# The steady round of a cross-attention kernel, its statements in another order

## The chip, the cores and the metric

The kernel runs on one core of a Trainium2 chip. The metric is the device time of one execution in microseconds (us). The time before is 1385.47 us, the median of three runs (1383.31 to 1385.71).

## What is computed

There are B = 64 sequences of 256 rows. Each has text rows of 512 values (`H_l`, the input x) and context rows of 384 values (`H_a`, the input ctx_768). All is float32. In the reference, cut to what matters:

```python
text_p  = einsum('bld,dh->blh', H_l, W_text)  + b_text
audio_p = einsum('bsd,dh->bsh', H_a, W_audio) + b_audio
Q = layer_norm(text_p, g1, beta1)
K = layer_norm(audio_p, g2, beta2)
alpha = softmax(einsum('blh,bsh->bls', Q, K) / sqrt(512))
H_hyper = einsum('bls,bsh->blh', alpha, audio_p)
H_hyper = einsum('blh,hk->blk', H_hyper, W_out) + b_out
return layer_norm(H_hyper + H_l, g_out, beta_out)
```

## The kernel before

**A pipeline of rounds.** One loop runs over the sequences, `for b in range(B - 2)`. Rounds 3 to 60 take its first branch (`if fast:`, L1315), the steady round; that branch is one list of some 140 calls, written out by hand, and it is all that the change touches. In it eight sequences are under way at once:

- b + 4 and b + 3: blocks of x and c are loaded (`load_c`, `load_x`), turned on VectorE (`turn_x`, `turn_c`), and sums of their blocks are made on GpSimd (`SumX` L293, `Sides` L321; each `.add(1)` is one GpSimd sum).
- b + 2: `k2` and `q2`, the projections to K and Q. Their variances, then `normalise` on ScalarE, then `store` to DRAM and `fetch` back in blocks of 32 x 32, so that the rows can be turned.
- b + 1: `k[b + 1].turn` and `q[b + 1].turn` on VectorE and `affine_keys` on ScalarE (gain and shift by column); `key_step(0)` to `(2)`, sums of key blocks on GpSimd.
- b: `at`: `affine_queries`, `query_step(0)` to `(3)` on GpSimd, the scores, their maxima, exponentials and the division, `store_e`.
- b - 1 and b - 2: `last` and `old`: the exponentials come back (`fetch_e`, `turn_e`) and are multiplied with the context (`context_one`, `context_two`); `y = old.o` multiplies with the output weights, and `plus_...`, `last_10`, `last_11`, `last_01`, `last_00` add x and leave the rows with their totals.
- b - 3: `settled`: the last layer norm. `totals` (L983, two GpSimd instructions on one column, the means `nm`), `deviation(0)`, `(1)` and `last_deviation` on ScalarE, then on VectorE, for each of two row tiles t, `shift(t)` (L1141, row plus mean, times gain) and `settle(t)` (L1152, row times 1/deviation, plus shift). These four each read two operands of 128 x 512 from SBUF and write SBUF. `done.store` sends the rows out.

**Fewer products.** The matrix products are written as block schemes with fewer multiplications, at the price of sums: `Fork` (L701) makes q by seven products, `Thirds` (L534) makes k and y by fifteen each, the scores take seven parts. So an accumulator in PSUM is used again and again: a product is added, ScalarE copies the state, VectorE writes the difference into another accumulator, more products follow. `k2` and `y` use the same accumulators M, L, T, U and N one after the other, and the same rooms in SBUF (`n1`, `t`, `m`, `n`, `u`, `d`); R and q1 to q3 are those of `Fork`. Some steps of the chain of `Thirds`: products `one` into N; `copy_n1` (ScalarE); `start_t` (VectorE, T from N); `three` into T; `copy_t`; `two` into M; `start_l0`, `start_l1` (L from M and t); `four`; `take_m`, `start_u` (U from M); `five`; `copy_n`, `copy_u`; `leave_middle`, `leave_ends`, `leave`; `middle_d`, `middle_sum` (GpSimd). `seed` puts the bias into M, `Fork.seed` into R. For the scores, `score_part(5)` writes where `add_p7(0)` has read, and `score_part(3)` where `add_p7(1)` has read.

**What sets the order.** The kernel is under a manual schedule: each engine executes its instructions in the order in which the statements issue them, and waits by one semaphore per engine for what other engines produce. So a list of statements is five queues: TensorE (PE), VectorE (DVE), ScalarE (ACT), GpSimd (POOL) and SyncE (SP). All loads and stores stand in SP's queue, and an issue there waits for its data and blocks those behind it. Buffers are few: the pool `once` has one of each tile (`kr`, `qr`, `zsum`, `ksum`, `qsum`, `e`), `work`, `blk`, `xin` and `cin` have two.

Helper lines that the profile names: L548 products of `Thirds`, L721 of `Fork`, L867 of the scores, L945 of the context; L532 the VectorE sums; L343 sums of `Sides` (`csum`, `zsum`), L314 of `SumX`, L849 `key_step`, L852 `query_step`, L990 `totals`; L518 affine, L1008 `deviation`, L479 and L787 `normalise` of k and q; L511 `turn` of k, L73 the loads in blocks, L489 `store` of k and q.

Of the kernel before, what the change touches and what calls it, by code (L numbers as in the profile page):

```python
# [22 lines left out]
def kernel(  # L23
# [20 lines left out]
    B, L, D = x.shape  # L44
# [24 lines left out]
    def squares(dst, src):  # L69

        v = src.rearrange("(b j) (q f) -> q j b f", j=SQ, q=NQ)
        for q in (0, 2, 1, 3):
            nc.sync.dma_start(dst[q * SQ : (q + 1) * SQ], v[q])  # L73
# [7 lines left out]
    def load_c(b):  # L81
        cq = blk.tile([P, S // SQ, DA // NQ], F32, tag="cq", name=f"cq_{b}")
        squares(cq, c[b])
        blocks[b] = [cq]

    def load_x(b):
        xq = blk.tile([P, L // SQ, D // NQ], F32, tag="xq", name=f"xq_{b}")
        squares(xq, x[b])
        blocks[b].append(xq)
# [5 lines left out]
    def load_x_rows(b):  # L95
        x_rows[b] = xin.tile([P, LT, D], F32, tag="x", name=f"x_{b}")
        nc.sync.dma_start(x_rows[b], x[b].rearrange("(t p) d -> p t d", p=P))

    def load_c_rows(b):
        c_rows[b] = cin.tile([P, ST, DA], F32, tag="c", name=f"c_{b}")  # L100
        nc.sync.dma_start(c_rows[b], c[b].rearrange("(t p) d -> p t d", p=P))
# [308 lines left out]
    def rstd_beside(var, n, by=1.0):  # L410

        log = small.tile([P, n], F32, tag=f"log{n}", name="log")
        nc.scalar.activation(log, var, AF.Ln, bias=eps, scale=by)
        r = small.tile([P, n], F32, tag=f"rstd{n}", name="rstd")
        nc.scalar.activation(r, log, AF.Exp, scale=-0.5)  # L415
        return [r[:, t : t + 1] for t in range(n)]
# [109 lines left out]
    def scales_of(a, b, var):  # L526

        r = rstd_beside(var, 4)
        a.r, b.r = r[:2], r[2:]
# [171 lines left out]
    class Fork(Projection):  # L701

        R, q1 = fork[0][:, :H2], fork[0][:, H2:]
        q2, q3 = fork[1][:, :H2], fork[1][:, H2:]
# [465 lines left out]
    def turn_x(b):  # L1170
        xT = work.tile([P, DC, L], F32, tag="xT", name=f"xT_{b}")
        turn(xT, blocks[b][1], DC)
        return xT

    def turn_c(b):
        cT = work.tile([P, AC, S], F32, tag="cT", name=f"cT_{b}")
        turn(cT, blocks[b][0], AC)
        return cT
# [7 lines left out]
    q, k, xT, cT, xs, cs, att = {}, {}, {}, {}, {}, {}, {}  # L1186
# [48 lines left out]
    wt_blocks = weight_sums(wt_sb, DC // 2, "wtsum")  # L1235
# [73 lines left out]
    for b in range(B - 2):  # L1309
        at = att[b] = att.get(b) or Attention(b)  # L1310
        settled, old, last = att.pop(b - 3, None), att.get(b - 2), att.get(b - 1)
# [3 lines left out]
        if fast:  # L1315
            k2 = k[b + 2] = Thirds("k", b + 2, cs.pop(b + 2), wa_blocks, ba_sb, ba_delta)
            q2 = q[b + 2]
            x_old = x_rows[b - 2]

            var = small.tile([P, 4], F32, tag="var4", name="var")  # L1320
            last.fetch_e()
            k2.one()
            old.context_two(0); old.context_two(1)
            if b + 4 < B: load_c(b + 4)
            k2.copy_n1()
            k2.start_t()
            old.copy_two()
            settled.totals()
            at.affine_queries(1)
            cT[b + 3] = turn_c(b + 3)  # L1330
            at.affine_queries(0)
            q2.six()
            old.start_products(n=1)
            y = old.o
            k2.three()
            k2.copy_t()
            k2.two()
            k2.start_l0()
            at.affine_queries(2)
            old.zsides.add(1)  # L1340
            q2.seven()
            k2.start_l1()
            at.query_sums()
            at.query_step(0)
            old.zsides.add(1)
            at.affine_queries(3)
            settled.deviation(0)
            k2.four()
            xT[b + 3] = turn_x(b + 3)
            k2.take_m()  # L1350
            q2.after_seven()
            settled.deviation(1)
            at.query_step(1)
            old.zsides.add(1)
            k2.start_u()
            k2.five()
            k2.copy_n()
            k2.copy_u()
            at.open_scores()
            q2.start_q3()  # L1360
            old.zsides.add(1)
            at.query_step(2)
            y.one()
            y.copy_n1()
            q2.step_r()
            q2.five()
            k2.leave_ends()
            old.zsides.add(1)
            y.seed()
            k2.leave_middle()  # L1370
            settled.last_deviation()
            k[b + 1].turn([0])
            k2.leave()
            k[b + 1].turn([1])
            y.start_t()
            at.score_part(1, 7)
            k2.square(var[:, 2:], [0])
            at.copy_p1()
            q2.after_five()
            y.two()  # L1380
            at.copy_p7()
            q[b + 1].turn()
            old.zsides.add(1)
            y.three()
            y.copy_t()
            load_x_rows(b - 1)
            y.start_l1()
            q2.four()
            q2.two()
            at.query_step(3)  # L1390
            cs[b + 3] = Sides(cT.pop(b + 3), "csum").add(0)
            cs[b + 3].add(1)
            last.turn_e()
            y.start_l0()
            k2.middle_d()
            settled.shift(1)
            at.score_part(6)
            at.add_p7(0)
            q2.three()
            settled.settle(1)  # L1400
            att[b + 1] = Attention(b + 1)
            att[b + 1].affine_keys(0)
            y.four()
            y.take_m()
            at.score_part(5)
            x_new = SumX(xT.pop(b + 3))
            x_new.add(1)
            att[b + 1].affine_keys(2)
            y.start_u()
            x_new.add(1)  # L1410
            y.five()
            k2.middle_sum()
            q2.square(var[:, :2], [1])
            at.add_p7(1)
            load_c_rows(b)
            att[b + 1].affine_keys(1)
            k2.square(var[:, 2:], [1])
            if done: done.store()
            done = settled
            y.plus_ends(x_old)  # L1420
            at.score_part(4)
            y.last_11()
            q2.square(var[:, :2], [0])
            cs[b + 3].add(1)
            at.score_part(3)
            att[b + 1].affine_keys(3)
            x_new.add(1)
            scales_of(q2, k2, var)
            at.score_part(2)
            k2.normalise([0])  # L1430
            k2.normalise([1])
            q2.normalise([0])
            k2.seed()
            cs[b + 3].add(1)
            if b + 4 < B: att[b + 1].key_sums()
            if b + 4 < B: att[b + 1].key_step(0)
            y.plus_middle(x_old, 1)
            if b + 4 < B: load_x(b + 4)
            cs[b + 3].add(1)
            y.plus_n0()  # L1440
            if b + 4 < B: att[b + 1].key_step(1)
            at.maxima()
            q2.normalise([1])
            Fork.seed()
            k2.store()
            last.context_one()
            settled.shift(0)
            at.exponentials([0])
            at.exponentials([1])
            y.last_10()  # L1450
            at.reciprocals()
            last.copy_one()
            y.plus_middle(x_old, 0)
            at.divide_e([0])
            q2.store()
            q3 = q[b + 3] = Fork(b + 3, x_new.of, wt_blocks)
            q3.one()
            x_new.add(1)
            y.last_01(x_old)
            k2.fetch()  # L1460
            cs[b + 3].add(1)
            at.divide_e([1])
            cs[b + 3].add(1)
            y.last_00()
            cs[b + 3].add(1)
            Fork.clear()
            q3.after_one()
            at.store_e()
            if b + 4 < B: att[b + 1].key_step(2)
            q2.fetch()  # L1470
            settled.settle(0)

            continue
        if b + 4 < B and b not in (1, 2):
# [6 lines left out]
        k2 = k[b + 2] = Thirds("k", b + 2, cs.pop(b + 2), wa_blocks, ba_sb, ba_delta)  # L1481
        if b < 3:
            q[b + 2] = Fork(b + 2, xs.pop(b + 2), wt_blocks)
        q2 = q[b + 2]
# [128 lines left out]
        var = small.tile([P, 4], F32, tag="var4", name="var")  # L1613
# [86 lines left out]
        if three and b > 1:  # L1700
            q3 = q[b + 3] = Fork(b + 3, xs.pop(b + 3), wt_blocks)
# [33 lines left out]
    settled, old, last = att[B - 5], att[B - 4], att[B - 3]  # L1735
    at = att[B - 2]
# [135 lines left out]
```

## Time and profile before

| What | Value |
|---|---|
| median of three runs | 1385.47 us (1383.31 to 1385.71) |
| the profiled execution's own time | 1384.61 us |
| its span, first to last instruction | 1382.8 us |
| PE busy in the span | 1360.8 us (98%) |
| PEld (weight loads) | 1245.9 us (90%) |
| DVE, ACT, POOL busy | 1195.5, 1166.7, 1159.2 us (86, 84, 84%) |
| packets of SP's queue, share of the 16 DMA engines' time | 80.9% |
| granted TensorE clock | 0.998 |

The profile is one execution, taken by the hardware profiler. A busy PE is not a PE at its peak: matmuls are pipelined and their ends are modelled, so a short wait between two of them can lie inside busy time. Every float32 matmul stands in the trace as two records, so a product of one matmul is "x2" and a pair of products is "x4". In the time lines, a row has the start in us, the length in us, the engine, the line, the operation, the tiles (output <- inputs), the shapes and the count of instructions merged into it; in brackets stands the idle time before it and what ended that. A group's row ends in busy time and mean ns. A row of the view by one line or one tile has min / median / max in ns.

### The profile page before, as it was taken

What the parts mean: (1) busy time and instruction counts of PE and PEld (TensorE: products, weight loads), DVE (VectorE), ACT (ScalarE), POOL (GpSimd) and SP (SyncE); (2) the same over time, 40 slices, a digit from 0 to 9 for tenths busy, and PEclk for the clock granted to TensorE, in tenths of its full rate; (3) what the DMA queues carried; (4) which work ended last, traced back from release to release, by engine and by line L of the source; (5) the groups of instructions that cost most, each with busy time, mean ns of one, the idle gap of its engine ahead of it and who ended that gap; (6) DMA issues with size and microseconds to landing.
All of it is one profiled execution on the core that took longest, in us unless ns stands there. A gap on an engine that the chain in (4) does not pass through costs nothing.

```text
span 1382.8 us, 28546 instructions
## 1 busy us (share of the span) xinstructions
PE 1360.8 (98%) x8125; PEld 1245.9 (90%) x8125; DVE 1195.5 (86%) x2733; ACT 1166.7 (84%) x3188; POOL 1159.2 (84%) x1838
## 2 busy tenths in 40 slices
PE   9999999999999999999999999999999999999997
PEld 5788999999999999999999999999999999999985
DVE  6758898899889899889998898998998988998857
ACT  5688888888888888888888888888888888888874
POOL 5669889889899889889888889889888898898844
PEclk9999999999999999999999999999999999999999
DMA  9787888888888888888888888888888888888772
GB/s 215 212 230 197 249 236 233 252 237 229 251 235 238 248 237 234 252 237 235 246 243 234 246 243 234 245 246 233 244 243 229 248 231 242 247 235 245 218 217 92
DMA packets 449107, 322.15 MB, mean 233 GB/s; under 512 B 153781, under 2 KB 381621, under 8 KB 448950
## 3 DMA queue, kind: packets, MB, share of 16 engines
q1 hardware_dynamic: 448854, 320.20, 80.9%
q8 instruction: 65, 1.06, 0.3%
q14 instruction: 92, 0.75, 0.2%
q10 hardware_dynamic: 96, 0.13, 0.0%
HBM read 203.57 MB, written 116.65 MB: 232 GB/s over the span
## 4 chain that ended last, share of the span: by engine, by line
PE 89%; DMA 3%; ACT 3%; DVE 3%; SPq 1%; issue 1%; DVEq 0%; POOL 0%; ACTq 0%
PE ps_f L721 26%; PE ps_m L548 16%; PE ps_sc L867 14%; PE ps_z L945 11%; PE ps_n L548 10%; PE ps_u L548 8%; PE ps_l L548 5%; DMA qd<-qr 1%; SPq L73 1%; DMA wo<-in_L_xattn_W_out_dram 1%; ACT junk L451 1%; DMA kd<-kr 0%; ACT junk L777 0%; DVE yr L1144 0%; DMA wt<-in_L_xattn_W_text_dram 0%
## 5 line engine op out<-in xcount | busy, mean ns | idle before, releaser
L1144 DVE SCALAR_TENSOR_TENSOR yr<-yr,nm,go 128x512 f32<-128x512 f32 x124 | 201.5, 1625 | 1.0 <-ACT junk L1025 1.0
L721 PE MATMUL ps_f<-wtsum,xsum 128*128 128x256 f32 x756 | 193.6, 379 | 0.5 <-DVE ps_f L532 0.5
L945 PE MATMUL ps_z<-eT,c 128*128 128x256 f32 x768 | 186.6, 379 | 0.2 <-ACT e L896 0.2
L343 POOL TENSOR_TENSOR csum<-csum,cT 128x256 f32<-128x256 f32 x310 | 178.6, 586 | 0.9
L343 POOL TENSOR_TENSOR zsum<-zsum,zT 128x256 f32<-128x256 f32 x305 | 170.5, 568 | 5.3
L849 POOL TENSOR_TENSOR ksum<-kT 128x512 f32<-128x512 f32 x58 | 73.9, 1274 | 97.9 <-ACT rstd L415 88.1
L721 PEld LDWEIGHTS ps_f<-wtsum,xsum 128*128 128x128 f32 x756 | 137.9, 190 | 15.3 <-DVE ps_f L532 1.2
L945 PEld LDWEIGHTS ps_z<-eT,c 128*128 128x128 f32 x768 | 138.5, 190 | 14.0 <-ACT e L896 0.6
L518 ACT ACTIVATE kT<-kT,columns 128x256 f32<-128x256 f32 x256 | 144.5, 593 | 2.6 <-DVE kT L511 1.5
L518 ACT ACTIVATE qT<-qT,columns 128x256 f32<-128x256 f32 x256 | 139.7, 596 | 2.2 <-DVE qT L76 2.2
L721 PE MATMUL ps_f<-wt,xT 128*128 128x256 f32 x504 | 129.4, 379 | 0.6 <-ACT ps_f L713 0.6
L532 DVE TENSOR_TENSOR ps_l<-ps_m,t 128x171 f32<-128x171 f32 x248 | 83.4, 336 | 52.7 <-PE ps_m L548 44.5
L867 PE MATMUL ps_sc<-kT,qT 128*128 128x128 f32 x928 | 122.3, 275 | 0.0
L867 PEld LDWEIGHTS ps_sc<-kT,qT 128*128 128x128 f32 x928 | 119.2, 192 | 3.0
L867 PE MATMUL ps_sc<-ksum,qsum 128*128 128x128 f32 x696 | 111.2, 282 | 0.4 <-DVE ps_sc L532 0.4
L721 PEld LDWEIGHTS ps_f<-wt,xT 128*128 128x128 f32 x504 | 95.5, 190 | 14.4 <-ACT ps_f L713 1.1
L867 PEld LDWEIGHTS ps_sc<-ksum,qsum 128*128 128x128 f32 x696 | 96.1, 191 | 11.4 <-DVE ps_sc L532 5.2
L990 POOL TENSOR_SCALAR nm<-totals 128x1 f32<-128x1 f32 x124 | 70.1, 580 | 38.7 <-DVE yr L691 38.7
L343 POOL TENSOR_TENSOR csum<-cT 128x256 f32<-128x256 f32 x124 | 96.6, 779 | 6.6 <-DVE cT L76 6.6
L343 POOL TENSOR_TENSOR zsum<-zT 128x256 f32<-128x256 f32 x122 | 72.6, 595 | 25.7 <-ACT zT L964 25.7
L314 POOL TENSOR_TENSOR xsum<-xT 128x256 f32<-128x256 f32 x124 | 88.3, 735 | 1.2 <-DVE xT L76 1.2
L1153 DVE SCALAR_TENSOR_TENSOR yr<-yr,rstd,beo 128x512 f32<-128x512 f32 x120 | 85.8, 717 | 0.0
(265 smaller groups left out, 4164.8 us busy)
## 6 DMA issues: line engine op xcount, KB each, us to landing
kd<-kr SPq DMA_DIRECT2D x64, 512.0 KB, 3.1
kq<-kd SPq DMA_DIRECT2D x256, 128.0 KB, 3.1
qd<-qr SPq DMA_DIRECT2D x64, 512.0 KB, 3.2
qq<-qd SPq DMA_DIRECT2D x256, 128.0 KB, 3.5
xq<-in_x_dram SPq DMA_DIRECT2D x252, 128.0 KB, 6.2
x<-in_x_dram SPq DMA_DIRECT2D x63, 512.0 KB, 4.5
out_dram<-yr SPq DMA_DIRECT2D x62, 512.0 KB, 6.2
cq<-in_ctx_dram SPq DMA_DIRECT2D x252, 96.0 KB, 2.4
```

Of the source, the lines that this page charges most:

```text
L314: self.engine.tensor_tensor(*step)
L343: nc.gpsimd.tensor_tensor(*step)
L518: nc.scalar.activation(self.T[:, k, :], self.T[:, k, :], AF.Identity, bias=bet[:, k : k + 1], scale=gam[:, k : k + 1],)
L532: nc.vector.tensor_tensor(o, i0, i1, op)
L548: nc.tensor.matmul(place, lhsT=self.sides.of[n], rhs=self.weights[n], start=(n == 14), stop=True, skip_group_check=True,)
L721: nc.tensor.matmul(place, lhsT=side, rhs=w, start=False, stop=True, skip_group_check=True)
L849: nc.gpsimd.tensor_tensor(*self.ksteps[n])
L867: nc.tensor.matmul(self.place(t, m), lhsT=self.qsides[n][:, c], rhs=self.ksides[n][:, c], start=False, stop=True, skip_group_check=True,)
L945: nc.tensor.matmul(ps, lhsT=c_rows[self.b][:, s, bass.ts(j, P)], rhs=self.eT[:, s, :], start=start, stop=(s == ST - 1), skip_group_check=True,
L990: nc.gpsimd.tensor_scalar(self.nm[:, j : j + 1], t[:, 0, j : j + 1], t[:, 1, j : j + 1], -1.0 / D, ALU.add, ALU.mult)
L1144: nc.vector.scalar_tensor_tensor(row, row, self.nm[:, t : t + 1], go_sb, ALU.add, ALU.mult)
L1153: nc.vector.scalar_tensor_tensor(self.y[:, t, :], self.y[:, t, :], self.r[t], beo_sb, ALU.mult, ALU.add)
```

## The change

The statements of the steady round stand in another order. None is added, removed or altered; nothing outside the branch is touched. Minus is the order before, plus the order after (unmarked lines kept their place in the comparison):

```diff
 x_old = x_rows[b - 2]
 
 var = small.tile([P, 4], F32, tag="var4", name="var")
-last.fetch_e()
 k2.one()
-old.context_two(0); old.context_two(1)
-if b + 4 < B: load_c(b + 4)
 k2.copy_n1()
 k2.start_t()
+xT[b + 3] = turn_x(b + 3)
+old.context_two(0); old.context_two(1)
 old.copy_two()
-settled.totals()
-at.affine_queries(1)
-cT[b + 3] = turn_c(b + 3)
-at.affine_queries(0)
-q2.six()
 old.start_products(n=1)
 y = old.o
+q2.seven()
+at.affine_queries(1)
 k2.three()
 k2.copy_t()
+at.open_scores()
+settled.totals()
 k2.two()
+at.affine_queries(0)
+q2.after_seven()
+k2.start_l1()
 k2.start_l0()
+settled.deviation(0)
+q2.six()
+last.fetch_e()
+old.zsides.add(1)
+q2.start_q3()
+settled.deviation(1)
+k2.four()
 at.affine_queries(2)
-old.zsides.add(1)
-q2.seven()
-k2.start_l1()
+at.affine_queries(3)
+q2.step_r()
+k2.take_m()
 at.query_sums()
 at.query_step(0)
 old.zsides.add(1)
-at.affine_queries(3)
-settled.deviation(0)
-k2.four()
-xT[b + 3] = turn_x(b + 3)
-k2.take_m()
-q2.after_seven()
-settled.deviation(1)
-at.query_step(1)
 old.zsides.add(1)
 k2.start_u()
 k2.five()
+settled.shift(0)
+q2.five()
+old.zsides.add(1)
 k2.copy_n()
 k2.copy_u()
-at.open_scores()
-q2.start_q3()
-old.zsides.add(1)
-at.query_step(2)
+settled.last_deviation()
+if b + 4 < B: load_c(b + 4)
+at.query_step(1)
 y.one()
 y.copy_n1()
-q2.step_r()
-q2.five()
+k[b + 1].turn([0])
+k2.leave_middle()
 k2.leave_ends()
+k2.leave()
+q2.after_five()
 old.zsides.add(1)
+k2.middle_d()
+at.score_part(1, 7)
+k[b + 1].turn([1])
 y.seed()
-k2.leave_middle()
-settled.last_deviation()
-k[b + 1].turn([0])
-k2.leave()
-k[b + 1].turn([1])
+at.copy_p7()
+at.query_step(2)
 y.start_t()
-at.score_part(1, 7)
+q2.three()
+at.copy_p1()
+old.zsides.add(1)
+at.query_step(3)
+y.three()
+q2.four()
+q[b + 1].turn()
+at.score_part(6)
+att[b + 1] = Attention(b + 1)
+att[b + 1].affine_keys(0)
+k2.middle_sum()
 k2.square(var[:, 2:], [0])
-at.copy_p1()
-q2.after_five()
+load_x_rows(b - 1)
+x_new = SumX(xT.pop(b + 3))
+x_new.add(1)
 y.two()
-at.copy_p7()
-q[b + 1].turn()
-old.zsides.add(1)
-y.three()
+cT[b + 3] = turn_c(b + 3)
+at.add_p7(0)
 y.copy_t()
-load_x_rows(b - 1)
+att[b + 1].affine_keys(3)
 y.start_l1()
-q2.four()
-q2.two()
-at.query_step(3)
+att[b + 1].affine_keys(1)
 cs[b + 3] = Sides(cT.pop(b + 3), "csum").add(0)
 cs[b + 3].add(1)
-last.turn_e()
+cs[b + 3].add(1)
 y.start_l0()
-k2.middle_d()
+q2.two()
 settled.shift(1)
-at.score_part(6)
-at.add_p7(0)
-q2.three()
-settled.settle(1)
-att[b + 1] = Attention(b + 1)
-att[b + 1].affine_keys(0)
+q2.square(var[:, :2], [1])
+q2.square(var[:, :2], [0])
+at.score_part(5)
+k2.square(var[:, 2:], [1])
+cs[b + 3].add(1)
+att[b + 1].affine_keys(2)
+if b + 4 < B: att[b + 1].key_sums()
+if b + 4 < B: att[b + 1].key_step(0)
+at.add_p7(1)
+settled.settle(0)
+scales_of(q2, k2, var)
 y.four()
-y.take_m()
-at.score_part(5)
-x_new = SumX(xT.pop(b + 3))
+k2.normalise([0])
+at.score_part(3)
+at.score_part(2)
 x_new.add(1)
-att[b + 1].affine_keys(2)
-y.start_u()
-x_new.add(1)
-y.five()
-k2.middle_sum()
-q2.square(var[:, :2], [1])
-at.add_p7(1)
-load_c_rows(b)
-att[b + 1].affine_keys(1)
-k2.square(var[:, 2:], [1])
 if done: done.store()
 done = settled
+q2.normalise([0])
+y.take_m()
+y.start_u()
+q2.normalise([1])
+cs[b + 3].add(1)
+cs[b + 3].add(1)
+last.turn_e()
+k2.normalise([1])
+at.score_part(4)
+x_new.add(1)
+at.maxima()
+at.exponentials([0])
+y.five()
+last.context_one()
+Fork.seed()
+q3 = q[b + 3] = Fork(b + 3, x_new.of, wt_blocks)
+q3.one()
+cs[b + 3].add(1)
+if b + 4 < B: load_x(b + 4)
 y.plus_ends(x_old)
-at.score_part(4)
-y.last_11()
-q2.square(var[:, :2], [0])
-cs[b + 3].add(1)
-at.score_part(3)
-att[b + 1].affine_keys(3)
 x_new.add(1)
-scales_of(q2, k2, var)
-at.score_part(2)
-k2.normalise([0])
-k2.normalise([1])
-q2.normalise([0])
-k2.seed()
-cs[b + 3].add(1)
-if b + 4 < B: att[b + 1].key_sums()
-if b + 4 < B: att[b + 1].key_step(0)
+at.exponentials([1])
+k2.store()
+load_c_rows(b)
 y.plus_middle(x_old, 1)
-if b + 4 < B: load_x(b + 4)
-cs[b + 3].add(1)
+last.copy_one()
+q2.store()
 y.plus_n0()
 if b + 4 < B: att[b + 1].key_step(1)
-at.maxima()
-q2.normalise([1])
-Fork.seed()
-k2.store()
-last.context_one()
-settled.shift(0)
-at.exponentials([0])
-at.exponentials([1])
 y.last_10()
+k2.fetch()
+y.last_11()
 at.reciprocals()
-last.copy_one()
+at.divide_e([1])
 y.plus_middle(x_old, 0)
 at.divide_e([0])
-q2.store()
-q3 = q[b + 3] = Fork(b + 3, x_new.of, wt_blocks)
-q3.one()
-x_new.add(1)
-y.last_01(x_old)
-k2.fetch()
-cs[b + 3].add(1)
-at.divide_e([1])
-cs[b + 3].add(1)
-y.last_00()
-cs[b + 3].add(1)
-Fork.clear()
-q3.after_one()
 at.store_e()
 if b + 4 < B: att[b + 1].key_step(2)
+y.last_01(x_old)
+k2.seed()
+Fork.clear()
 q2.fetch()
-settled.settle(0)
+y.last_00()
+q3.after_one()
+settled.settle(1)
+cs[b + 3].add(1)
```

On each engine the count of instructions stays the same. In the queues, as they stand after: `settled.shift(0)` follows `k2.start_u` on VectorE, `settled.shift(1)`, `add_p7(1)` and `settled.settle(0)` stand between `y.start_l0` and `y.take_m`, and `settled.settle(1)` is the last of the round (before: `shift(1)` and `settle(1)` around `add_p7(0)`, ahead of `y.take_m`; `shift(0)` after `maxima`, `settle(0)` last). On GpSimd `totals` stands behind the first `zsum` sum. On SyncE `load_c_rows` stands behind `k2.store` (before: ahead of `done.store`). On ScalarE the second `k2.normalise` comes behind both of `q2`.

## The prediction

> **What bounds the kernel now.** I read the busy shares first, then rounds against each other in the stretches view, then the engines' time lines of one round, then who waited for whom. Times below that begin at 0 are counted from the first matmul of `k2.one` in a round, at 751.50 us in the round that I use most.
>
> ```profile
> 125.66:1313.40 1187.74, 1187.68 (x7297) 1107.72 (x7296) 1063.88 (x2451) 1034.24 (x2851) 1046.48 (x1651) 1.00 0.83 240
> 751.50:772.37 20.87, 20.87 (x129) 19.44 (x128) 18.78 (x44) 18.15 (x51) 18.31 (x30) 1.00 0.85 240
> 772.37:792.83 20.46, 20.46 (x129) 19.43 (x128) 17.74 (x44) 18.14 (x51) 18.95 (x30) 1.00 0.85 246
> ```
>
> The columns are length, then busy time of PE, PEld, DVE, ACT and POOL, granted clock, DMA share and GB/s. The first row is 57 of the 58 steady rounds, 20.84 us each. PE is busy throughout, at full clock. The reader is to see that two neighbouring rounds of the same code, with the same matmuls, differ by 0.41 us, and that the shorter one has 1.04 us less of DVE. So a busy PE hides stalls. The PE time line says where:
>
> ```profile
> 763.82 1.03 PE L721 MATMUL ps_f<-wt,xsum 128*128 128x256 f32 x4
> 764.69 0.45 PE L548 MATMUL ps_u<-wao_thirds,zsum 128*128 128x171 f32 x2
> ...
> 765.56 0.74 PE L548 MATMUL ps_l<-wao_thirds,zT 128*128 128x171 f32 x4
> 766.19 0.71 PE L867 MATMUL ps_sc<-ksum,qsum 128*128 128x128 f32 x4
> 766.74 0.75 PE L548 MATMUL ps_n<-wao_thirds,zsum 128*128 128x171 f32 x4
> 767.47 0.85 PE L548 MATMUL ps_m<-wao_thirds,zT 128*128 128x171 f32 x4
> ```
> ```profile
> 786.43 0.74 PE L548 MATMUL ps_l<-wao_thirds,zT 128*128 128x171 f32 x4
> 787.01 0.61 PE L867 MATMUL ps_sc<-ksum,qsum 128*128 128x128 f32 x4
> 787.45 0.75 PE L548 MATMUL ps_n<-wao_thirds,zsum 128*128 128x171 f32 x4
> ```
>
> From start to start, a pair of products costs 0.87 us at 256 columns, 0.58 at 171 and 0.44 at 128. In the long round the scores take 0.63 to begin and 0.55 to pass, and `y.five` waits 0.73 - 0.58 = 0.15 and more for its M products. Both places wait for DVE:
>
> ```profile
> 763.29 2.64 DVE L1144 SCALAR_TENSOR_TENSOR yr<-yr,nm,go 128x512 f32<-128x512 f32 x1
> 765.85 0.29 DVE L532 TENSOR_TENSOR ps_sc<-ps_sc,sc 128x128 f32<-128x128 f32 x1
> 766.05 0.74 DVE L1153 SCALAR_TENSOR_TENSOR yr<-yr,rstd,beo 128x512 f32<-128x512 f32 x1
> ```
> ```profile
> 762.76 0.56 POOL L648 TENSOR_TENSOR kr<-u,d 128x171 f32<-128x171 f32 x1
> 763.26 0.74 POOL L343 TENSOR_TENSOR csum<-csum,cT 128x256 f32<-128x256 f32 x1
> 763.95 0.74 POOL L314 TENSOR_TENSOR xsum<-xsum,xT 128x256 f32<-128x256 f32 x1
> 764.63 0.75 POOL L343 TENSOR_TENSOR csum<-csum,cT 128x256 f32<-128x256 f32 x1
> ```
> ```profile
> 784.15 1.26 DVE L1144 SCALAR_TENSOR_TENSOR yr<-yr,nm,go 128x512 f32<-128x512 f32 x1
> ```
>
> `settled.shift(1)` takes 2.64 us in the long round and 1.26 in the short one. It reads two SBUF rows, and it ends 0.55 us after the third POOL sum that began beside or after it: less than the 0.74 that the like `settle` takes with POOL idle. So it waited for POOL's whole run, and `add_p7(0)`, which the scores wait for, stood behind it. **The stall of the round is one DVE instruction shut out by POOL.** The sum of it: 1187.74 - 57 x 20.46 = 21.5 us.
>
> **The change part by part.** No instruction is added or removed; PE's set of matmuls is the same, so its floor stays 20.46 a round. What can change is the 21.5 us, down to nothing or up. I lay out the new PE order by the three prices: `k2.one` 0, `context_two` 0.58, `q2.seven` 1.44, `k2.three` 2.31, `k2.two` 2.60, `q2.six` 3.18, `k2.four` 4.04, `k2.five` 5.49, `q2.five` 6.94, `y.one` 7.81, scores 1 and 7 8.39, `q2.three` 9.28, `y.three` 10.15, `q2.four` 10.44, score 6 11.30, `y.two` 11.75, `q2.two` 12.33, score 5 13.20, `y.four` 13.65, scores 3, 2, 4 15.10, `y.five` 16.45, `context_one` 17.90, `q3.one` 19.63. Then I ask of each wait whether its producer is done. Most chains (copy, subtract, product) now have another product group between their ends, as `score_part(6)` to `score_part(5)`, which were 2 apart and now have `y.two` and `q2.two` (1.4 us) between them. I cost those at nothing: PE's other groups cover them, and uncovered the price is the stall of before, some 0.1 to 0.4 a round. What decides are the four two-row DVE instructions, in their new places beside POOL.
>
> *`shift(0)`, now behind `k2.start_u`.* Its rows:
>
> ```profile
> 757.07 0.34 DVE L532 TENSOR_TENSOR ps_u<-ps_m,m 128x171 f32<-128x171 f32 x1
> 758.41 0.51 DVE L532 TENSOR_TENSOR kr<-ps_m,n 128x342 f32<-128x342 f32 x1
> 759.23 1.29 DVE L511 STREAM_TRANSPOSE kT<-kq 128x512 f32<-128x512 f32 x2
> 760.67 0.42 DVE L532 TENSOR_TENSOR ps_f<-ps_f,s 128x256 f32<-128x256 f32 x1
> ```
> ```profile
> 753.61 0.73 POOL L343 TENSOR_TENSOR zsum<-zT 128x256 f32<-128x256 f32 x1 [0.20 <-ACT zT L964]
> 756.47 0.73 POOL L852 TENSOR_TENSOR qsum<-qT 128x256 f32<-128x256 f32 x1
> 757.16 0.87 POOL L343 TENSOR_TENSOR zsum<-zsum,zT 128x128 f32<-128x128 f32 x2
> 757.99 0.73 POOL L852 TENSOR_TENSOR qsum<-qsum,qT 128x256 f32<-128x256 f32 x1
> ```
> ```profile
> L990 POOL TENSOR_SCALAR nm<-totals x124: 261/267/935, 106.4 to 1367.4; 128x1 f32<-128x1 f32 x124
> ```
> ```profile
> 754.41 0.28 ACT L596 COPY t<-ps_u 128x171 f32<-128x171 f32 x1
> 754.60 1.09 ACT L518 ACTIVATE qT<-qT,columns 128x256 f32<-128x256 f32 x2
> 757.17 0.20 ACT L1008 ACTIVATION_READ_ACCUMULATOR junk<-yr,nm 128x1 f32 x1
> ```
>
> The second M product of `k2.four` is through at about 5.1 (4.04, three products, the drain of one); `take_m` and `start_u`, 0.34 each, bring `shift(0)` to 5.8. POOL starts `zsum` at 2.11 as before (its input is still the copy behind `context_two`). Before, seven sums ran from 753.61 to 757.99, 4.38 us; now `query_step(1)` (0.69) leaves that stretch and the two `nm` (0.26 each, nothing beside them) enter: it ends at 6.3. So `shift(0)` asks during the fourth or fifth short `zsum`. What comes next on POOL is `query_step(1)`, which needs `affine_queries(3)` of ACT: from 2.8, ACT's work of 754.41 to 757.37 (2.96) and one more affine (0.5) end at 6.25. POOL is then free, or nearly, at the moment when DVE asks. Before had the same situation, a DVE request inside a short sum:
>
> ```profile
> 770.62 0.86 DVE L1144 SCALAR_TENSOR_TENSOR yr<-yr,nm,go 128x512 f32<-128x512 f32 x1
> ```
> ```profile
> 770.06 0.88 POOL L343 TENSOR_TENSOR csum<-csum,cT 128x128 f32<-128x128 f32 x2
> 770.89 0.91 POOL L343 TENSOR_TENSOR csum<-cT 128x128 f32<-128x128 f32 x1
> ```
>
> There DVE lost 0.12 us and POOL's next sum, 0.44 alone, took the wait. I take this row, the nearest: `shift(0)` done by 6.8. The other end is that of 763.29, 1.9 us lost. Behind it stand `k.turn([0])`, `leave_middle`, `leave_ends` and `after_five` (0.65, 0.82 for the pair, 0.42), and `q2.three` at 9.28 waits for the last: `shift(0)` may end as late as 7.4 at no cost.
>
> *`shift(1)` and `settle(0)`, now between `y.start_l0` and `y.take_m`*, 13.3 to 14.9. POOL's third `csum` sum runs into that; then `key_step(0)` must wait for ACT's last `affine_keys`. Before, such a wait was there in every round, and the settle at 766.05 ran inside it:
>
> ```profile
> POOL ksum L849 <- ACT rstd L415: 88.1, 56, 1.8
> ```
>
> 1.57 us a round. ACT does that affine after all four squares, and `q2.square([0])` cannot start before `q2.two` ends at 13.2, so POOL sits idle till about 15.3. `shift(1)` waits for one sum at most, `add_p7(1)` is done by 14.7, and score 3 needs it at 15.1. Gain: the stall of before.
>
> *`settle(1)`, now last*, about 21.0, asks during `key_step(2)`. One lost sum more is 0.45 us; `start_t` behind it also waits for `copy_n1`, and `k2.three` is due at 22.8. I cost it at nothing; without that cover it is 0.2 a round.
>
> *SP's queue.* `load_c_rows` moves behind `k2.store`, and the second `k2.normalise`, which that store waits for, now comes last of the four.
>
> ```profile
> 767.98 0.38 SPq L489 DMA_DIRECT2D kd<-kr  x1
> 770.06 0.38 SPq L489 DMA_DIRECT2D qd<-qr  x1
> 770.84 2.18 SPq L73 DMA_DIRECT2D kq<-kd  x4
> ```
> ```profile
> kq<-kd SPq DMA_DIRECT2D x256, 128.0 KB, 3.1
> ```
>
> The k store therefore goes where the q store went (18.56 instead of 16.48, as that one waited for all four), the k fetch 2.86 behind it at 21.4, its last part at 23.1, landed at 26.2, which is 5.7 of the next round. `k.turn([0])` wants it at 6.8. Before, it was there 4 us early; now 1. The q fetch behind it is as much later and keeps about half a us to `q.turn` at 9.3, but `q.turn` and `turn_c` may run 1.4 us late before `add_p7(0)` is missed by score 5. The other loads keep over 2 us.
>
> The sum: 1384.61 (the profiled execution) - 21.5 = 1363.1; the median of the runs is 0.9 above that execution, which makes 1364.0. I take off 0.5 for part of the stalls of the first steady round, and say **1363.5 us**.
>
> The Trainium skill (SBUF — State Buffer, section "Who interferes with whom") says that a DVE instruction with two SBUF inputs and a GpSimd one that reads SBUF shut each other out, and that the later one blocks until the first has finished. The rows agree on the shutting out and differ on its length: 2.64 us spans three POOL instructions. By the rule `shift(0)` could lose 0.5 us at most, and the first rival below would have no chance.
>
> **The rivals.** *A, as forecast* (0.62): 1361 to 1367. *B, part of it* (0.13): some requests lose a sum or two, or `Fork.seed` and `start_t` come 0.1 to 0.3 late: 1367 to 1383. *C, a new stall as long as the old* (0.05): 1383 to 1388. *D, slower by the lock* (0.13): at 5.8, `query_step(1)` follows the short sums without a break, and POOL keeps the port as at 763.29. From 6.3 POOL then has work to 9.7 without a wait (four sums of 0.5 to 0.69 and two of 0.41); there `middle_sum` waits for `leave_ends`, which stands behind `shift(0)`, and lets it in. It decides from the second lost sum on: `shift(0)` then ends near 8.0, `q2.three` is 0.6 late, 57 x 0.6 = 34 us, 1397; shut out to the end it is 2.8 a round, 1523. For it: 763.29, in nearly every round. Against it: 770.62, whose short sums are the likelier likeness, and the wait for ACT. *E, slower by the fetch* (0.07): if the `c` load and the q store in front of `kq` hold it 2.5 us longer than 3.1, `k.turn([0])` starts at 8.2, `q2.three` 0.8 late: 1409 again.
>
> **How the numbers follow.** A and B are faster by over 0.2% (2.8 us, about what a measurement of this kernel tells from no change): 0.75. C is the same: 0.05. D and E: 0.20. Range 1360.5 to 1390: it leaves out most of D and E and a little below.
>
> **What would show it.** Right: rounds of 20.46 in the stretches view; no L1144 over 1.5 us; PE groups at their prices. Wrong: L1144 over 2 us behind `start_u` (D), DVE idle before L511 for `kq` (E), PE gaps at `q2.three`, score 3 or `k2.three`.

## The result, and the profile after

The changed kernel takes **1367.19 us** (median of four runs, 1366.51 to 1367.78) against 1385.47 before; the ratio is 0.9871 with a 95% interval of 0.9854 to 0.9888. It is faster, by 18.3 us; the forecast was 1363.5. The profiled execution took 1367.78 us, with a span of 1365.9 and a granted clock of 0.998.

The stretches view (length; busy time of PE, PEld, DVE, ACT, POOL with counts; clock, DMA share, GB/s), first for rounds 4 to 60, then for two neighbours, then for round 3, the first steady round:

```profile
123.24:1295.86 1172.62, 1169.97 (x7298) 1106.46 (x7297) 1027.54 (x2451) 1029.53 (x2851) 1060.04 (x1653) 1.00 0.88 243
247.48:267.94 20.46, 20.46 (x129) 19.43 (x128) 18.04 (x44) 18.02 (x51) 18.59 (x30) 1.00 0.87 244
267.94:289.45 21.51, 20.92 (x129) 19.25 (x128) 17.53 (x43) 18.24 (x51) 18.78 (x30) 1.00 0.86 235
...
102.11:123.24 21.13, 20.85 (x129) 19.35 (x128) 17.37 (x42) 18.10 (x51) 19.65 (x30) 1.00 0.54 146
```

The same round 3 before:

```profile
102.48:125.66 23.18, 21.37 (x129) 19.45 (x128) 18.82 (x42) 18.66 (x52) 20.20 (x32) 1.00 0.66 182
```

The 57 rounds went from 1187.74 to 1172.62 us (-15.12), round 3 from 23.18 to 21.13 (-2.05), everything else by +0.34: together the -16.83 between the two profiled executions. 43 of the 57 rounds are now at 20.46 (before: 5). DVE is busy 36 us less in the same 2451 instructions.

What was one DVE instruction of 2.64 us is now this, DVE and then POOL of one round in the time line (start, length):

```profile
466.94 0.74 DVE L1144 SCALAR_TENSOR_TENSOR yr<-yr,nm,go 128x512 f32<-128x512 f32 x1
467.60 0.29 DVE L532 TENSOR_TENSOR ps_sc<-ps_sc,sc 128x128 f32<-128x128 f32 x1
467.80 1.02 DVE L1153 SCALAR_TENSOR_TENSOR yr<-yr,rstd,beo 128x512 f32<-128x512 f32 x1
```
```profile
465.41 0.73 POOL L343 TENSOR_TENSOR csum<-cT 128x256 f32<-128x256 f32 x1 [0.31 <-DVE cT L76]
466.22 2.04 POOL L343 TENSOR_TENSOR csum<-csum,cT 128x256 f32<-128x256 f32 x2
469.23 1.27 POOL L849 TENSOR_TENSOR ksum<-kT 128x512 f32<-128x512 f32 x1 [0.96 <-ACT kT L518]
```

`shift(1)` gets the port between two `csum` sums (below, "gets the port" and "is let in" mean that DVE goes ahead after a wait for POOL). The later sum now bears the wait (2.04 us for two sums of 0.73), and `add_p7(1)` follows in time. Over all rounds, the group of both `shift` (minimum / median / maximum in ns) reads:

```profile
L1144 DVE SCALAR_TENSOR_TENSOR yr<-yr,nm,go x116: 741/744/1310, 129.0 to 1303.4; 128x512 f32<-128x512 f32 x116
```

**What is left.** 1172.62 - 57 x 20.46 = 6.40 us, in 14 rounds. The round of 21.51 shows it; DVE, then PE:

```profile
273.68 0.74 DVE L1144 SCALAR_TENSOR_TENSOR yr<-yr,nm,go 128x512 f32<-128x512 f32 x1
276.17 0.71 DVE L511 STREAM_TRANSPOSE kT<-kq 128x512 f32<-128x512 f32 x1 [1.75 <-DMA kq<-kd]
276.80 0.30 DVE L532 TENSOR_TENSOR kr<-ps_u,u 128x171 f32<-128x171 f32 x1
277.02 0.50 DVE L532 TENSOR_TENSOR kr<-ps_m,n 128x342 f32<-128x342 f32 x1
277.44 0.42 DVE L532 TENSOR_TENSOR ps_f<-ps_f,s 128x256 f32<-128x256 f32 x1
```
```profile
277.92 1.13 PE L721 MATMUL ps_f<-wt,xsum 128*128 128x256 f32 x4 [0.54 <-DVE ps_f L532]
```

`k.turn([0])` waits 1.75 us for the k fetch, `q2.after_five` stands behind it, and `q2.three` on PE starts late. The waits view and the view of DMA issues (packets' size, median us from issue to landing), of the kernel after:

```profile
DVE kT L511 <- DMA kq<-kd: 20.7, 24, 1.8
```
```profile
kq<-kd SPq DMA_DIRECT2D x256, 128.0 KB, 3.8
```

A part of the fetch takes 3.8 us where it took 3.1. The last part lands at 6.2 to 6.6 us of the next round as a rule (in a few rounds up to 7.3), and in eleven rounds at 7.6 to 8.1; a landing before some 7.3 costs PE next to nothing. These eleven rounds are 6.1 of the 6.4 us. In a 1.95 us stretch of the late round, the view by queue has one packet that most rounds lack, 16 KB of instructions (the last column is the share of the time of the 16 DMA engines; 6.0% of 16 x 1.95 is 1.9 us of one engine); all such packets of the execution are the second row:

```profile
q8 instruction: 1, 0.02, 6.0%
```
```profile
q8 instruction: 66, 1.08, 0.4%
```

All eleven late rounds have such a packet begun between 3.7 and 5.7 us of the round, while the last parts of `kq` are under way. Four other rounds have one there and are not late, so the packets come with the late fetches but are not shown to cause them.

### The profile page after: what moved, and what is told of

Same layout as the page of the kernel before. It is cut to its first block, busy times and chain, and to the rows that moved or that the text cites. A ratio compares the mean times of both kernels' runs of the same rounds, so it can differ in the third digit from the quotient of the medians.

```text
span 1365.9 us, 28598 instructions
## 1 busy us (share of the span) xinstructions
PE 1342.8 (98%) x8125; PEld 1244.8 (91%) x8125; DVE 1157.5 (85%) x2733; ACT 1161.8 (85%) x3188; POOL 1171.5 (86%) x1838
## 4 chain that ended last, share of the span: by engine, by line
PE 78%; DMA 7%; ACT 6%; DVE 3%; issue 2%; POOL 2%; SPq 1%; DVEq 0%; ACTq 0%; POOLq 0%
PE ps_f L721 23%; PE ps_m L548 13%; PE ps_sc L867 11%; PE ps_z L945 9%; PE ps_n L548 8%; PE ps_u L548 7%; PE ps_l L548 4%; DMA qd<-qr 2%; DMA kq<-kd 2%; DMA kd<-kr 1%; DMA qq<-qd 1%; ACT qr L787 1%; SPq L73 1%; ACT junk L777 1%; ACT junk L451 1%
## 5 line engine op out<-in xcount | busy, mean ns | idle before, releaser
L343 POOL TENSOR_TENSOR csum<-csum,cT 128x256 f32<-128x256 f32 x310 | 195.5, 640 | 9.9
L343 POOL TENSOR_TENSOR zsum<-zsum,zT 128x256 f32<-128x256 f32 x305 | 196.4, 653 | 5.3
L518 ACT ACTIVATE qT<-qT,columns 128x256 f32<-128x256 f32 x256 | 145.2, 593 | 2.2 <-DVE qT L76 2.2
L1153 DVE SCALAR_TENSOR_TENSOR yr<-yr,rstd,beo 128x512 f32<-128x512 f32 x120 | 119.6, 998 | 0.0
L867 PEld LDWEIGHTS ps_sc<-ksum,qsum 128*128 128x128 f32 x696 | 100.6, 191 | 6.0
L867 PE MATMUL ps_sc<-ksum,qsum 128*128 128x128 f32 x696 | 105.9, 275 | 0.0
L511 DVE STREAM_TRANSPOSE kT<-kq 128x512 f32<-128x512 f32 x122 | 85.4, 701 | 23.3 <-DMA kq<-kd 20.7
L777 ACT ACTIVATE junk<-ps_f 128x512 f32<-128x512 f32 x126 | 74.3, 590 | 36.2 <-PE ps_f L721 35.9
L1144 DVE SCALAR_TENSOR_TENSOR yr<-yr,nm,go 128x512 f32<-128x512 f32 x124 | 102.9, 831 | 1.0 <-ACT junk L1025 1.0
L76 DVE STREAM_TRANSPOSE qT<-qq 128x1024 f32<-128x1024 f32 x64 | 79.5, 1242 | 18.2 <-DMA qq<-qd 17.4
```

The source lines that it names most:

```text
L76: nc.vector.transpose(dst.rearrange("p k (b j) -> p b k j", j=SQ), src.rearrange("p b (k i) -> p b k i", k=chunks),)
L343: nc.gpsimd.tensor_tensor(*step)
L511: nc.vector.transpose(self.T.rearrange("p k (q t j) -> p t q k j", t=self.nt, j=SQ)[:, t], self.sq[:, t * NQ : (t + 1) * NQ].rearrange("p ...
L518: nc.scalar.activation(self.T[:, k, :], self.T[:, k, :], AF.Identity, bias=bet[:, k : k + 1], scale=gam[:, k : k + 1],)
L777: nc.scalar.activation(junk, fork[t], AF.Square, scale=1.0 / math.sqrt(H), accum_out=self.var[:, t : t + 1],)
L867: nc.tensor.matmul(self.place(t, m), lhsT=self.qsides[n][:, c], rhs=self.ksides[n][:, c], start=False, stop=True, skip_group_check=True,)
```

## The experiments

Theory 1 at the outset was that of the prediction: the 0.41 us a round is `shift(1)` shut out by POOL's sums. Its rival 2: the gain comes from the wider spacing of the chains on PE.

| Kernel | median us | ratio to before, 95% interval |
|---|---|---|
| e1 before, two DVE statements moved | 1385.75 | 1.0 (0.999 to 1.0009) |
| e1b the same two, to other places | 1367.28 | 0.9876 (0.9862 to 0.9889) |
| e6 before, one POOL sum moved | 1363.80 | 0.9849 (0.9835 to 0.9862) |
| e8 before, another POOL sum moved (a pause) | 1364.85 | 0.9851 (0.9834 to 0.9867) |
| e8c the same sum, without a pause | 1385.48 | 0.9994 (0.9985 to 1.0003) |
| e9 before, pause 8 sums ahead | 1363.64 | 0.9836 (0.9821 to 0.9851) |
| e9b before, pause 11 sums ahead | 1380.57 | 0.9956 (0.9939 to 0.9973) |
| e2, e2b after, two POOL sums moved | 1369.75, 1369.83 | 0.9884, 0.9885 (0.9869 to 0.9902) |
| e4 after, `k.turn` later | 1364.14 | 0.9844 (0.9829 to 0.9858) |
| e3 after, load of c early | 1365.05 | 0.9857 (0.9843 to 0.987) |
| e7 after, both | 1362.63 | 0.9839 (0.9826 to 0.9852) |

**e1.** The kernel before, with

```diff
-settled.shift(1)
...
-settled.settle(1)
...
 y.start_u()
+settled.shift(1)
...
 settled.settle(0)
+settled.settle(1)
```

> The order before, with two statements moved: settled.shift(1) behind y.start_u, where GpSimd waits for the last affine_keys, and settled.settle(1) to the end of the round. Theory 1 (the old stall was this one VectorE instruction shut out by a run of GpSimd sums): rounds of 20.46 us, 1363 to 1368 us. Rival 2 (the gain of the new order comes from the wider spacing of its product chains): less than a third of the gain, above 1379 us.

Measured 1385.75: a miss. But the old stall was gone and a new one stood elsewhere. DVE and PE of e1 around a round's start:

```profile
481.17 1.34 DVE L1153 SCALAR_TENSOR_TENSOR yr<-yr,rstd,beo 128x512 f32<-128x512 f32 x2
482.43 0.33 DVE L532 TENSOR_TENSOR ps_u<-ps_n,n 128x171 f32<-128x171 f32 x1
```
```profile
481.75 1.03 PE L721 MATMUL ps_f<-wtsum,xsum 128*128 128x256 f32 x4
482.91 0.53 PE L548 MATMUL ps_u<-wa_thirds,csum 128*128 128x171 f32 x2
483.27 0.74 PE L548 MATMUL ps_m<-wa,csum 128*128 128x171 f32 x4
```

Two settles now stand ahead of `start_t`, which `k2.three` waits for: PE starts it 1.16 us after the group before, 0.29 over its price of 0.87, and loses 0.07 more behind it. I had put the second settle where the round has no room. By its own ranges e1 spoke for rival 2; what it shows is that removing one stall and adding another cancel, which says nothing on theory 1 as such, so e1b put the two statements inside the round:

```diff
-settled.shift(1)
...
 at.add_p7(0)
+settled.shift(1)
...
-settled.settle(1)
...
 y.take_m()
+settled.settle(1)
```

> The kernel before with the same two DVE statements moved as in the first experiment, but to places inside the same half of the round: shift(1) behind add_p7(0), settle(1) behind the take_m of the output product; the round's boundary keeps one settle, as in the kernel before. In the first experiment the old stall was gone (shift(1) 0.74 us) and a new one of 0.37 us stood at the round's start, where the second settle of 0.67 us held up the copy of the key product's first part. Theory 1 with that reading: the gain that the first experiment lost comes back, rounds of 20.46 to 20.55 us, 1363 to 1370 us. Rival 2 (DVE has no room for the two in before's order, wherever they stand): 1380 to 1390 us.

1367.28: two statements of DVE's queue give the whole gain, and the spacing of all the other chains is not needed. Theory 1 held, though `shift(1)` still lost one sum here (1.68 us on the median, 1.39 to 1.76 in rounds 4 to 60): it asks late in POOL's run and waits to its end, but `add_p7(0)` no longer stands behind it.

**e2, e2b.** What lets DVE in? In the kernel after, each `csum` sum of the three waits for the one ahead of it, and POOL pauses 0.08 us there. e2 puts other sums into those pauses, e2b puts the same sums behind (moved up from behind `score_part(2)` and `score_part(4)`):

```diff
 cs[b + 3].add(1)
+x_new.add(1)
 cs[b + 3].add(1)
+x_new.add(1)
 y.start_l0()
...
 at.score_part(2)
-x_new.add(1)
...
 at.score_part(4)
-x_new.add(1)
```
```diff
 cs[b + 3].add(1)
+x_new.add(1)
+x_new.add(1)
 att[b + 1].affine_keys(2)
...
 at.score_part(2)
-x_new.add(1)
...
 at.score_part(4)
-x_new.add(1)
```

> The order after, with two SumX sums taken from behind key_step(0) and put between the first three csum sums, so that no sum follows directly on the one it reads and GpSimd runs without a break from 11.7 to about 15.2. Theory 1a (GpSimd keeps the port through a whole run without breaks): settled.shift(1) takes 2.2 us or more in most rounds, score 3 is about 0.8 late, 1400 to 1425 us. Rival 1b (VectorE waits for the one GpSimd instruction that is under way): settled.shift(1) takes 1.3 at most, within 3 us of the order after (1367).

> The same two SumX sums moved ahead of key_step(0), but behind the three csum sums, which still follow each other directly with a break of 0.08 us between. GpSimd is as long at work as with the sums interleaved. Theory 1a (VectorE gets the port in the breaks): settled.shift(1) stays at 0.74 to 1.3 us, within 3 us of the order after. Rival (what counts is only how long GpSimd has work): as slow as with the sums interleaved, 1400 or more.

Theory 1a fell, at least for sums this soon after a pause (DVE asks during the second or third): `shift(1)` still took no more than 1.33 us. Of the 2.6 us more than the kernel after, the longest rounds show the cause, late fetches again: of k, and in two rounds of e2 and one of e2b of q, which `q.turn` waits for. POOL in e2: the sum at 466.70 runs, DVE asks at 466.94 and gets the port at its end, though the next sum was ready; that one takes 1.18.

```profile
466.94 1.03 DVE L1144 SCALAR_TENSOR_TENSOR yr<-yr,nm,go 128x512 f32<-128x512 f32 x1
```
```profile
466.70 0.72 POOL L343 TENSOR_TENSOR csum<-csum,cT 128x256 f32<-128x256 f32 x1
467.39 1.18 POOL L314 TENSOR_TENSOR xsum<-xsum,xT 128x256 f32<-128x256 f32 x1
```

So sums without a pause between them let DVE in here and shut it out in the kernel before. **e6** asked whether one pause is enough in before's own place; only POOL's order changes:

```diff
-x_new.add(1)
...
 cs[b + 3].add(1)
+x_new.add(1)
 if b + 4 < B: att[b + 1].key_sums()
```

> The kernel before with one change on POOL alone: the third xsum sum (the one at 12.46 us of a round) goes behind the csum sum that followed it, so that the run under shift(1) is csum, csum (which needs the one ahead of it), xsum. No DVE, PE, ACT or SP statement moves. Theory 1 (the 0.41 us per round is shift(1) shut out by this run, and it gets the port where one sum has to wait for the one ahead of it): shift(1) takes 0.75 to 1.3 us instead of 2.65, the rounds go to 20.46 us, 1363 to 1368 us. Rival 2 (shift(1) merely stands in the wrong place of DVE's order, or the run as a whole shuts it out whatever its order): shift(1) stays over 2 us and the time stays at 1383 to 1388. Between them (1368 to 1383): shift(1) is short but settle(1), next behind it, is shut out in its place.

1363.80: one statement of POOL gives at least what the whole change gives (the two intervals overlap a little). DVE asks at 464.99, and is let in where the second `csum` has to wait for the first:

```profile
464.99 1.25 DVE L1144 SCALAR_TENSOR_TENSOR yr<-yr,nm,go 128x512 f32<-128x512 f32 x1
```
```profile
464.97 1.85 POOL L343 TENSOR_TENSOR csum<-csum,cT 128x256 f32<-128x256 f32 x2
466.78 1.18 POOL L314 TENSOR_TENSOR xsum<-xsum,xT 128x256 f32<-128x256 f32 x1
```

But e2 had shown that the pause needn't be where DVE asks. Call a row of POOL instructions without a pause between them a run. I listed, over all kernels so far, the ends of sums at which DVE was waiting and POOL did not pause, by the number of sums that POOL had done in its run: let in up to the 7th, as a rule shut out from the 15th. Theory 5 is that the length of the run decides. **e8** with its control **e8c** test it without touching the three sums:

```diff
 k2.middle_d()
+k2.middle_sum()
...
-k2.middle_sum()
```
```diff
 x_new.add(1)
+k2.middle_sum()
...
-k2.middle_sum()
```

> The kernel before with one other change on POOL alone: the sum kr (the one at 11.27 us of a round) goes directly behind the difference d that it needs (9.38), so that POOL pauses 0.08 us there, four sums ahead of the request of shift(1). The three sums under shift(1) stay csum, xsum, csum in the order of the kernel before, without a pause among them. In the runs so far DVE got the port at the next end of a sum where POOL's run since its last pause was 7 sums or shorter, and in the kernel before did not (two ends lost in 53 rounds) where it was the 15th sum or later. Theory 5 (the length of POOL's run without a pause decides): shift(1) takes 0.75 to 1.5 us, rounds of 20.46, 1363 to 1368 us. Rival 6 (these three sums in this order shut DVE out, whatever stood before them): shift(1) stays over 2 us, 1383 to 1388.

> The control: the same sum kr moved by one place only, between the two xsum sums, where what it needs is long done and POOL doesn't pause. The run of POOL stays without a pause from 3.6 us to the request, as in the kernel before. Theory 5 and rival 6 both: shift(1) stays at 2.6 us, 1383 to 1388. A third possibility (any reorder of POOL moves the request off the place where it loses): under 1375.

Both as theory 5 has it. POOL and DVE of e8; after `d` (462.14) it pauses 0.08 us, and DVE gets in at the end of the third sum of the new run:

```profile
461.57 0.57 POOL L645 TENSOR_TENSOR d<-n 128x171 f32<-128x171 f32 x1
462.22 0.55 POOL L648 TENSOR_TENSOR kr<-u,d 128x171 f32<-128x171 f32 x1
462.73 1.42 POOL L314 TENSOR_TENSOR xsum<-xT 128x256 f32<-128x256 f32 x2
464.11 1.19 POOL L343 TENSOR_TENSOR csum<-csum,cT 128x256 f32<-128x256 f32 x1
465.26 1.17 POOL L314 TENSOR_TENSOR xsum<-xsum,xT 128x256 f32<-128x256 f32 x1
```
```profile
463.98 0.73 DVE L1144 SCALAR_TENSOR_TENSOR yr<-yr,nm,go 128x512 f32<-128x512 f32 x1
```

And e8c, the same sums without the pause:

```profile
470.00 0.57 POOL L648 TENSOR_TENSOR kr<-u,d 128x171 f32<-128x171 f32 x1
470.51 0.75 POOL L314 TENSOR_TENSOR xsum<-xT 128x256 f32<-128x256 f32 x1
471.20 0.74 POOL L343 TENSOR_TENSOR csum<-csum,cT 128x256 f32<-128x256 f32 x1
471.88 0.74 POOL L314 TENSOR_TENSOR xsum<-xsum,xT 128x256 f32<-128x256 f32 x1
472.57 0.74 POOL L343 TENSOR_TENSOR csum<-csum,cT 128x256 f32<-128x256 f32 x1
```
```profile
471.22 2.64 DVE L1144 SCALAR_TENSOR_TENSOR yr<-yr,nm,go 128x512 f32<-128x512 f32 x1
```

One more rival would be the moment of the request: in most rounds of before and of e8c it comes 0.02 to 0.05 us ahead of a sum's end, perhaps too late for that end, in e8 some 0.17 us ahead. But in six rounds of before it comes 0.41 to 0.60 us ahead of the end, and is shut out all the same (2.33 to 2.52 us). One of them, DVE and then POOL:

```profile
241.94 2.52 DVE L1144 SCALAR_TENSOR_TENSOR yr<-yr,nm,go 128x512 f32<-128x512 f32 x1
```
```profile
241.81 0.73 POOL L343 TENSOR_TENSOR csum<-csum,cT 128x256 f32<-128x256 f32 x1
```

**e9, e9b** move the pause farther back:

```diff
 at.query_step(2)
+at.query_step(3)
...
-at.query_step(3)
```
```diff
 at.query_step(1)
+at.query_step(2)
...
-at.query_step(2)
```

> The kernel before with another single POOL change that makes a pause farther from the request: the last query_step goes directly behind the one whose result it needs, so that POOL pauses 0.08 us at about 7.2 us of the round; from there to the request of shift(1) at 11.8 it runs 7 to 8 sums without a pause, the three under shift(1) as in the kernel before. Theory 5 (the length of the run decides; let in at 7 sums or fewer so far, shut out at 14 or more): it says nothing yet between 7 and 14; if DVE is let in, 1363 to 1368 and shift(1) at 0.75 to 1.5 us, and the limit lies above 7; if not, 1383 to 1388 and the limit is right there. Any time between would speak against a limit in the count of sums.

> The same with the third query_step directly behind the second: the pause comes at about 5.7 us of the round, and POOL runs 10 to 11 sums without a pause up to the request. Theory 5: let in (1363 to 1368) if the limit lies above 11 sums, shut out (1383 to 1388) if below; if the run with 8 sums is shut out, this one must be too.

e9: let in, 1363.64; of rounds 4 to 60, in 49 at the first end, in 8 at the second. e9b is a miss in its time, which lies between the two: its rounds are 20.72, because the third `query_step` now stands ahead of two `zsum` sums that it stood behind. These two end 0.8 us later, and `y.one`, the first group that multiplies `zsum`, takes 0.81 us to pass instead of 0.58. Its own question is answered by the rows of `shift(1)`: let in at the first end in 49 rounds, shut out to the end of the run in 8. Two rounds of e9b:

```profile
533.37 1.12 DVE L1144 SCALAR_TENSOR_TENSOR yr<-yr,nm,go 128x512 f32<-128x512 f32 x1
...
554.09 2.51 DVE L1144 SCALAR_TENSOR_TENSOR yr<-yr,nm,go 128x512 f32<-128x512 f32 x1
```

So the limit is not a fixed count: a request in the 8th sum of the run is let in everywhere, at the first end or the second; one in the 12th in 49 of 57 rounds; one in the 16th (in a few rounds the 14th or 15th) in 5 of 58 (before) and in none of 58 (e8c).

**e4, e3, e7** are on the 6.1 us of late rounds (theory 3: `k.turn` waits for the k fetch). e4 puts each `k.turn` four statements later (the expectation of e7 says two), e3 puts the load of c back ahead of `done.store`, e7 does both:

```diff
-k[b + 1].turn([0])
...
 q2.after_five()
+k[b + 1].turn([0])
...
-k[b + 1].turn([1])
...
 y.start_t()
+k[b + 1].turn([1])
```
```diff
+load_c_rows(b)
 if done: done.store()
...
-load_c_rows(b)
```

> The order after, with k.turn([0]) moved behind q2.after_five and k.turn([1]) behind y.start_t, so that VectorE has nothing due behind a late k fetch. Theory 3 (what is left over 20.46 in 15 of the rounds is VectorE waiting for the last part of the k fetch): the fetch still lands late in such rounds, no PE gap at q2.three, 1361 to 1364 us. Rival 4 (the rest comes from shift(0) or from GpSimd): no change, 1366 to 1368.

> The changed kernel with one SP statement put back to where it was: the load of c ahead of the store of the finished rows, so that it is not in flight with the k fetch. Theory 3 (the 5 us of late rounds are k.turn waiting for a k fetch that takes 3.7 us beside the load of c and the q store, and longer when an instruction fetch falls on it): the fetch takes about 2.6 to 3.1 us, the last part lands at 5.2 to 5.8 us of the next round, late ones stay below the 7.3 at which the stall begins, 1361 to 1365 us. Rival 4 (the c load has no part in it, the instruction fetch alone decides): same as the changed kernel within 1.5 us, 1366 to 1369.

> The changed kernel with both cures of the late k fetch: k.turn later by two statements each, and the load of c put back ahead of the store. Theory 3: no round waits for the k fetch, but the run with k.turn later had about 1 us of other small gaps left, so 1362 to 1364.5 us, at most 1.5 us better than that run. Rival 5 (the load of c in its old place brings a wait of its own, for c or the q fetch): 1365 to 1370.

e4: 1364.14. In its profiled execution, the fastest of its four (1362.29), the 57 rounds are 1.05 us over the floor instead of 6.40, while a part of the fetch still takes 3.8 us. So it is `k.turn`'s place that made the lateness cost. e3: the fetch back at 2.7 us, so the c load had a part in its length; 1365.05, just past the upper end of theory 3 and below the 1366 of rival 4. It moved a part of the wait, as the rows now leave late. The issues and the waits of e3:

```profile
kq<-kd SPq DMA_DIRECT2D x256, 128.0 KB, 2.7
```
```profile
DVE kT L511 <- DMA kq<-kd: 5.6, 8, 1.2
DVE yr L691 <- DMA out_dram<-yr: 5.0, 6, 1.6
```

e7 at 1362.63, within the range of theory 3, is the fastest kernel of all, faster than both before and after; its lead on e4, e6 and e9 is within what repeated runs scatter.

## Why the prediction was right, and where it was off

**The floor and the stall** were right: rounds of 20.46, and the 0.41 us is one DVE instruction shut out. e6, e8 and e9 show it in the kernel before with only POOL's order changed, e8c with the counter-check.

**`shift(0)`** was to lose 0.12 and end by 6.8; it asks at 5.73, takes 0.74 and loses nothing in nearly every round. POOL is not free at that moment, which the prediction had assumed; but it pauses 0.08 us ahead of the `zsum` sum under which the request falls (5.44 to 5.89 us of the round), and lets DVE in at that sum's end. The sum in the round of 21.51, whose `shift(0)` at 273.68 stands above:

```profile
273.38 0.45 POOL L343 TENSOR_TENSOR zsum<-zsum,zT 128x128 f32<-128x128 f32 x1
```

For the same reason rival D, which took POOL's run from there as unbroken, did not come. **`shift(1)`**, one sum at most: right (0.74 to 1.31). The reason given, POOL's idle time ahead of `key_step(0)`, is not the one that counts: the request comes before it, and the fresh run of `csum` lets it in. **`settle(1)`** at no cost: right, the rounds stay at 20.46.

**The k fetch is the step that was off.** The prediction let each part take 3.1 us, the row of before, though the c load and the q store now go out right ahead of it, and put the last landing at 5.7. It took 3.8, landed at 6.2 to 6.6, and in eleven rounds at 7.6 to 8.1. As a rule 0.7 to 1.1 us were left to the point from which it costs, much like the prediction's margin of 1; in the eleven rounds none was left, and 6.1 us were lost, as e4 shows by taking nearly all of them away. This is rival E's mechanism at a seventh of its price (1409 - 1363.5 = 45.5), with both of its signs, DVE idle before L511 and PE gaps at `q2.three`, but in eleven rounds and not in all: the prediction reckoned with one duration of the fetch and not with its spread. So the time, 1367.19, lies 0.2 us past the range of the forecast's own rival A and in that of B, whose causes (lost sums, late `Fork.seed`) are not what happened.

From 1363.5 to 1367.2: +6.4 (the 14 rounds over the floor), -1.55 (round 3 gave 2.05, not 0.5), +0.34 (the rest), -1.49 (the median lay 0.59 below the profiled execution, not 0.9 above). The terms of -1.55 and -1.49 are luck: the forecast had no reason for them, and without them the miss would have been 6.7 us instead of 3.7.

**The rule cited** (the Trainium skill, SBUF — State Buffer, section "Who interferes with whom"): that the later instruction blocks until the first has finished describes e2, e8 and 49 of the 57 rounds of e9 (0.73 to 1.33 us, the next POOL sum bearing the wait); in the other eight of e9 one sum more went ahead (1.36 to 1.38 us). It does not hold behind a long unbroken run of POOL: there, in before, two or more further sums went ahead of DVE in 53 of 58 rounds. Had I taken it for a rule, I would have had no account of the 2.64 us at all. (Where the prediction says that by this rule "the first rival below" would have no chance, rival D is meant, not A.)

**Open:** why a long run keeps the port; whether its sums count or its time, as both grew together (at the request the run is some 1.8 us old in e8, 4.5 in e9, 6.3 in e9b and 8.9 in before); and what decides the mixed rounds at the 12th sum (in before, four of the five rounds that were let in lie 8 rounds apart). Open too is whether the instruction packets cause the late fetches or only come with them; their place wasn't varied. They can't be the only cause: in e2 the longest wait for the k fetch came in a round with no such packet between the fetch's issue and its landing (wait, then issues):

```profile
358.81 0.71 DVE L511 STREAM_TRANSPOSE kT<-kq 128x512 f32<-128x512 f32 x1 [2.22 <-DMA kq<-kd]
```
```profile
kq<-kd SPq DMA_DIRECT2D x4, 128.0 KB, 5.1
```

## What to carry to other kernels

When a two-operand VectorE instruction takes a multiple of its time, look at what GpSimd did before it, not only beside it: a single GpSimd sum placed so that it must wait for the one ahead of it (0.08 us), eight sums or fewer before the request, gave here what a new order of some 140 statements gave. Before moving an instruction, ask what it stands in front of at the new place; the second settle of e1 ate the whole gain. And a fetch that lands some 0.7 to 1.1 us early as a rule is late in some rounds: give its consumer the slack of the worst round, where moving it costs nothing.

## What the runs showed of the hardware

A VectorE instruction with two operands in SBUF, which waits for GpSimd, was let in at the end of a GpSimd sum while the run since the last pause was short (8 sums: in 49 of 57 rounds at the first end, else at the second). Behind a long run it waited for several sums (16: in 53 of 58 rounds of before and in all of e8c, where `shift` took 2.3 to 3.2 us). The view by queue counts packets of 16 KB of instructions in the time of the 16 DMA engines that move the data; one took 1.9 us of one engine, in a round whose k fetch ended at 8.1 us instead of 6.2 to 6.6.
